# Softmax maxima written out by ScalarE instead of VectorE, in a decoder block on one Trainium2 core

## The chip, the cores and the metric

The kernel runs on one core of a Trainium2 chip. The core has five engines with queues of their own, each worked in order: TensorE (PE in the profile; PEld is its loading of weights), VectorE (DVE), ScalarE (ACT), GpSimd (POOL) and SyncE (SP), which here only issues DMAs. The metric is the device time of one execution in microseconds. Each profile comes from one further execution, whose own time is given beside it.

## What is computed

One decoder block on x, 32 batches of 128 tokens of width 256, in float32. The reference, cut to its frame:

```python
x = x + attn(layernorm(x), Wq, bq, Wk, bk, Wv, bv, Wo, bo)     # causal linear attention, 16 heads of 16
x = x + xattn(layernorm(x), ctx, ctx, Wq, Wk, Wv)              # softmax attention to a context of 128 tokens
x = x + ffn(layernorm(x), ...)                                 # silu gate, two gelu layers of 1024
```

The change is in the second line, where `attn = jax.nn.softmax(q k^T / 4)` over the 128 context tokens, for 16 heads. A softmax subtracts the maximum of each row of scores before the exponential. The kernel works on transposed scores (context token on the partition, query token along the free axis), so the negated maxima, which come out with the query token on the partition, have to be turned and then added to all 128 partitions.

## The kernel before, in words

**Work.** The batches go in 16 pairs. Each pair passes through linear attention (functions `a_...`, called "a" below) and, three pairs later (`SKEW` = 3), through softmax attention (`b_...`, called "b"). The feed-forward block (FFN) then works on 8 blocks of 4 batches, with weights kept in SBUF, and its matmuls in two parts (high and low, so that two float32r products give float32). All PE, ACT, DVE and POOL instructions stand in the order in which the program calls them (`tc.manual_schedule`, with all four engines in `ORDERED`); nothing is reordered.

**Order.** Lists written out by hand set that order. Each entry names a function, a pair offset and, where it applies, which batch of the pair (0 or 1, the first or second half). Functions are generators: each mention runs one up to its next `yield`. So `b_turn_maxima` stands twice for each half: at the first mention the PE transpose is emitted, at the second what comes after the `yield`, which is the part that the change touches. The lists in order of time: `head` and three `first` lists (linear attention alone), `both` (12 steps: linear attention of one pair and softmax attention of an earlier one), then `close`, `begins`, `alone` and `last` (one step each: the last four pairs of softmax attention), and `rest`. There are 32 halves: 24 in `both` and 2 in each of the four late lists. In `begins`, `alone` and `last`, `beside` and `settle` weave in the first FFN block: `beside` emits the matmuls of one FFN piece (`ffn_gate` L233 with a silu on ACT at L238, `ffn_gelu` L244 with a gelu at L248), and `settle` their ACT, DVE and POOL work, followed by `load_exp` (L81), a one-column Exp whose purpose is to bring back the table of Exp: so a table load to silu or gelu and a table load back (charged to L81) stand around each of these activations.

**One half of softmax attention.** `b_maxima` (L594): scores `sm` (L397), their negated maxima `nm` by two DVE reductions (L603), split into a float32r high part and a rest in the tile `z` (L607, L608). In `z`, group g (of four) has 32 columns; of these, columns 0 to 3 hold the high parts of its four heads i, 4 to 7 the rests, and the others are zero. `b_turn_maxima` (L611): PE transposes `z` into the PSUM tile `pz` (L613), so row 32g+i and row 32g+4+i hold head (g, i). These must go to four places: `mT` (L615) has four slots of 128 columns, and slot i keeps only the rows of head i, the others being zero. The column i of `sel` (L329) is one at the rows of head i and zero elsewhere. `b_scores` (L621): the scores once more, into `se` (L397), then per group a matmul with a matrix of ones (L628), whose 32 rows add up the rows of `mT` and so put minus the maximum on all 128 partitions; then ACT takes the exponential into `pr` (L639). `b_weighted` multiplies by the values (`pf`, L413), DVE turns the result (`fb`, L430), and `b_out` adds it to x (`pot` L652, `oc` L655).

**Other lines named below.** `phi` (L489) makes the features of linear attention: two Exp `e` (L495) and two Relu `r` (L497) on ACT. `b_queries`, `b_keys` and `b_values` copy projections out of PSUM on ACT (`qb` L571; `kb` L580 and L583; `vb` L592). `a_scores` masks scores on DVE (`at` L536); `a_values` writes `va` (L521) on DVE; `divided` turns `fa` and `fb` (L430). `ffn_input` casts `xh` on ACT (L188).

**Score banks.** The scores `sa` (linear attention), `sm` and `se` share two PSUM tiles (`ps_s`). The next scores can only be written when the last reader of the ones before is done: DVE's reduction after `sm`, ACT's exponential after `se`, DVE's masking after `sa`. The four other PSUM banks (`ps_m`) are given to all other tiles of the attention and, in the late lists, to the first FFN block.

Of the kernel before, what the change touches and what calls it, by code (L numbers as in the profile page):

```python
# [11 lines left out]
AF = mybir.ActivationFunctionType  # L12
ALU = mybir.AluOpType
# [3 lines left out]
P = 128  # L17
B, S, D = 32, 128, 256
# [26 lines left out]
def decoder_block_kernel(  # L45
# [14 lines left out]
    nc = tc.nc  # L60
# [207 lines left out]
    with tc.manual_schedule(engines=ORDERED):  # L268
# [7 lines left out]
        def buffer(shape, dtype, tag, name, **kw):  # L276
            side = att_a if tag in A_TAGS else att_b
            return side.tile(shape, dtype, tag=tag, name=name, **kw)
# [38 lines left out]
        sel = tiny.tile([P, 4], F32, name="sel")  # L317
# [16 lines left out]
        def bank(name):  # L334
            return ps_m.tile([P, 4, S], F32, tag="m", name=name)
# [275 lines left out]
        def b_turn_maxima(m, j):  # L611
            pz = bank("pz").rearrange("p a s -> p (a s)")[:, :S]
            nc.tensor.transpose(pz, Bs[m].pop(("z", j)).rearrange("p g r -> p (g r)"), ident)  # L613
            yield
            mT = buffer([P, 4, S], F32R, tag="mT", name="mT")  # L615
            nc.vector.tensor_tensor(
                mT, pz.unsqueeze(1).to_broadcast([P, 4, S]), sel.unsqueeze(2).to_broadcast([P, 4, S]), ALU.mult
            )
            Bs[m]["mT", j] = mT

        def b_scores(m, j):  # L621
# [60 lines left out]
        def settle():  # L682
# [42 lines left out]
        both = [  # L725
            (a_transpose, 1), (b_maxima, 0, 0), (b_transpose, 1), (b_values, 1), (b_maxima, 0, 0),
            (b_out, -1, 1), (a_scores, 0, 0), (a_transpose, 1), (b_transpose, 1), (b_turn_maxima, 0, 0),
            (a_scores, 0, 0), (b_out, -1, 1), (a_keys, 1), (b_values, 1), (b_turn_maxima, 0, 0),
            (w_load, 0), (norms, 0), (a_out, -1, 1), (b_scores, 0, 0), (a_keys, 1), (b_queries, 1),
            (a_out, -1, 1), (b_scores, 0, 0), (b_queries, 1), (b_maxima, 0, 1), (norms, 0),  # L730
            (b_weighted, 0, 0), (b_out, -1, 1), (b_queries, 1), (norms, 0), (b_maxima, 0, 1),
            (a_keys, 1), (b_load, 2), (a_weighted, 0, 0), (a_scores, 0, 1), (b_turn_maxima, 0, 1),
            (a_bias, 1), (norms, 0), (norms, 0), (b_weighted, 0, 0), (a_scores, 0, 1),
            (b_turn_maxima, 0, 1), (a_weighted, 0, 0), (b_weighted, 0, 0), (a_queries, 1),
# [318 lines left out]
```

## Time and profile before

| | |
|---|---|
| time, median of 3 runs | 1091.75 us (1090.9 to 1091.82) |
| time of the profiled execution | 1090.88 us |
| its span | 1088.7 us |
| granted TensorE clock, mean | 0.999 |
| multiply `mT` (L616) on DVE | 32 times, 681 ns in the mean, 21.8 us |
| transpose `pz` (L613) on PE | 32 times, 320 ns in the mean |
| negated maxima `nm` (L603) on DVE | 64 times, 1217 ns in the mean |
| exponentials `pr` (L639) on ACT | 64 times, 1020 ns in the mean |
| table loads on ACT | 15 at L238, 11 at L248, 12 at L81, 1283 ns each |

The span reaches from the first to the last instruction of the profiled execution; the time has some 2 us around it. A group in the profile is given as its line, engine, operation, tiles out<-in, shapes and count, then busy us, mean ns of one, and the idle time of the engine just before it with what ended it. In a timeline, the first number is the start in us from the start of the span, the second how long the row lasts, and brackets hold idle time before it with its releaser. The ends of matmuls are modelled. The stages lie as follows: `both` to about 370 us, `close` to 391, `begins` from there to 414, `alone` to 434, `last` to 455, then `rest` and the FFN blocks up to the end.

### The profile page before, as it was taken

The numbers are of one execution on the slowest core, as the hardware profiler recorded it, in microseconds if no ns is written. First come the engines' busy times: TensorE is split into PE (matmuls) and PEld (weight loads), VectorE is DVE, ScalarE is ACT, GpSimd is POOL, SyncE is SP. The second block draws the span as 40 slices with busy tenths as digits, with TensorE's granted clock in tenths as the row PEclk, the third lists the DMA queues.
The fourth block names the chain that finished last, engine by engine and source line by source line (L and its number), as shares of the span: only waits on it lengthen the run. The fifth ranks groups of instructions, "written<-read, shape, count | busy, mean of one in ns | idle before, by whom it ended". The sixth has DMA issues, their size and how long they took to land.

```text
span 1088.7 us, 19303 instructions
## 1 busy us (share of the span) xinstructions
PE 1076.1 (99%) x7990; PEld 875.4 (80%) x7990; DVE 598.7 (55%) x1209; ACT 377.8 (35%) x594; POOL 406.4 (37%) x649
## 2 busy tenths in 40 slices
PE   8999999999999999999999999999999999999998
PEld 6777777777777777778888888888888888888887
DVE  5888888888888876523433433433433432422422
ACT  3244444444444359822322322322312312312311
POOL 5554555545444446552312312312312312312311
PEclk9999999999999999999999999999999999999999
DMA  7011101111111000051011010011011000000000
GB/s 266 2 30 31 31 30 31 31 34 46 30 31 30 11 11 2 20 193 35 25 39 34 25 39 35 25 39 37 23 39 39 20 30 20 11 10 20 11 1 23
DMA packets 26542, 39.21 MB, mean 36 GB/s; under 512 B 2512, under 2 KB 18640, under 8 KB 26448
## 3 DMA queue, kind: packets, MB, share of 16 engines
q1 hardware_dynamic: 22000, 26.09, 7.3%
q0 software_dynamic: 4032, 11.54, 3.5%
q8 instruction: 65, 1.06, 0.4%
q10 hardware_dynamic: 416, 0.28, 0.1%
q14 instruction: 29, 0.24, 0.1%
HBM read 33.71 MB, written 4.19 MB: 35 GB/s over the span
## 4 chain that ended last, share of the span: by engine, by line
PE 94%; DVE 2%; POOL 1%; DMA 1%; issue 0%; ACT 0%; SPq 0%; POOLq 0%; DVEq 0%; ACTq 0%
PE ph L224 51%; PE pp L368 10%; PE py L877 6%; PE pf L413 5%; PE pv L376 5%; PE sa L397 4%; PE sm L397 3%; PE se L397 3%; PE pw L376 2%; PE pt L357 1%; PE pot L652 1%; DMA H<-in_h2T_dram 1%; PE se L628 1%; PE pz L613 1%; PE pt L213 1%; DVE at L536 1%
## 5 line engine op out<-in xcount | busy, mean ns | idle before, releaser
L189 DVE TENSOR_TENSOR gl<-hg,gh 128x512 fp32r<-128x512 f32 x125 | 86.9, 695 | 334.3 <-POOL gh L188 331.3
L248 ACT ACTIVATE hg<-ph,col 128x512 f32<-128x512 f32 x128 | 88.3, 690 | 362.5 <-PE ph L224 362.4
L188 POOL CAST gh<-hg 128x512 fp32r<-128x512 f32 x128 | 79.5, 621 | 357.9 <-ACT hg L248 357.9
L224 PE MATMUL ph<-gh,H 128*128 128x512 f32 x512 | 199.3, 389 | 0.5 <-POOL gh L188 0.5
L224 PE MATMUL ph<-sh,H 128*128 128x512 f32 x512 | 199.6, 390 | 0.0
L224 PE MATMUL ph<-gl,H 128*128 128x512 f32 x512 | 199.3, 389 | 0.2 <-DVE gl L189 0.2
L224 PE MATMUL ph<-sl,H 128*128 128x512 f32 x512 | 199.2, 389 | 0.0
L224 PEld LDWEIGHTS ph<-gh,H 128*128 128x128 f32 x512 | 96.1, 188 | 20.7 <-POOL gh L188 0.9
L224 PEld LDWEIGHTS ph<-gl,H 128*128 128x128 f32 x512 | 96.1, 188 | 20.5 <-DVE gl L189 0.5
L224 PEld LDWEIGHTS ph<-sh,H 128*128 128x128 f32 x512 | 96.1, 188 | 20.4 <-issue 0.5
L224 PEld LDWEIGHTS ph<-sl,H 128*128 128x128 f32 x512 | 96.1, 188 | 19.9
L224 PE MATMUL ph<-xh,W 128*128 128x512 f32 x256 | 100.7, 394 | 0.0
L224 PE MATMUL ph<-xl,W 128*128 128x512 f32 x256 | 99.8, 390 | 0.0
L603 DVE TENSOR_REDUCE nm<-sm 128x8 f32<-128x1024 f32 x64 | 75.2, 1217 | 17.9 <-PE sm L397 17.9
L188 POOL CAST sh<-hs 128x512 fp32r<-128x512 f32 x64 | 58.7, 917 | 68.6 <-DVE hs L240 68.6
L536 DVE TENSOR_TENSOR at<-sa,causal 128x1024 f32<-128x1024 f32 x64 | 74.5, 1206 | 14.6 <-PE sa L397 11.9
L639 ACT ACTIVATE pr<-se 128x1024 f32<-128x1024 f32 x64 | 62.0, 1020 | 29.6 <-PE se L628 29.6
L240 DVE SCALAR_TENSOR_TENSOR hs<-ph,col,sil 128x512 f32<-128x512 f32 x64 | 47.9, 749 | 41.3 <-PE ph L224 21.0
L238 ACT ACTIVATE sil<-ph,col 128x512 f32<-128x512 f32 x64 | 44.1, 690 | 74.9 <-PE ph L224 74.8
L495 ACT ACTIVATE e<-pp,col 128x256 f32<-128x256 f32 x64 | 26.9, 471 | 123.7 <-PE pp L368 92.7
L877 PE MATMUL py<-W,gh 128*128 128x256 f32 x256 | 62.6, 285 | 0.0
L877 PE MATMUL py<-W,gl 128*128 128x256 f32 x256 | 62.0, 283 | 0.0
(132 smaller groups left out, 1812.1 us busy)
## 6 DMA issues: line engine op xcount, KB each, us to landing
x<-in_x_dram SPq DMA_DIRECT2D x16, 256.0 KB, 5.5
cT<-in_ctxT_dram SPq DMA_DIRECT2D x16, 256.0 KB, 2.8
H<-in_h1T_dram POOLq DMA_DIRECT2D x8, 512.0 KB, 3.8
H<-in_h2T_dram POOLq DMA_DIRECT2D x8, 512.0 KB, 7.7
out_dram<-y SPq DMA_DIRECT2D x32, 128.0 KB, 1.7
raw<-in_h1T_dram SPq DMA_DIRECT2D x16, 256.0 KB, 2.7
raw<-in_h2T_dram SPq DMA_DIRECT2D x16, 256.0 KB, 2.6
WA<-in_wattn_dram SPq DMA_DIRECT2D x4, 256.0 KB, 4.8
```

The source lines that it names most:

```text
L188: (high_engine.copy if high_engine is nc.scalar else high_engine.tensor_copy)(high, t)
L189: lows.append(lambda: low_engine.tensor_tensor(low, t, high.bitcast(F32), ALU.subtract))
L224: nc.tensor.matmul(pp, lhsT=w[:, k, ts(c, P)], rhs=parts[p], start=(k == 0 and p == 0), stop=(k == len(src) - 1 and p == 1),)
L248: nc.scalar.activation(t, pp, AF.Gelu, scale=col[:, c_scale + c : c_scale + c + 1])
L368: nc.tensor.matmul(pp[:, c, :], lhsT=w[:, d, ts(c, P)], rhs=src[:, d, :], start=(d == 0), stop=(d == DC - 1))
L376: nc.tensor.matmul(pp, lhsT=src[:, d, :], rhs=w[:, d, :], start=(d == 0), stop=(d == DC - 1))
L397: nc.tensor.matmul(sc[g // 2][:, g % 2, 2 * c : 2 * c + 2, :], lhsT=loaded[32 * g : 32 * g + 32, c, ts(j, S)], rhs=streamed[32 * g : 32 * ...
L413: nc.tensor.matmul(pf[32 * g : 32 * g + 32, i, :], lhsT=v[:, 8 * (i // 2) + 2 * g + i % 2, :], rhs=weights[g // 2][:, g % 2, i, :], start= ...
L536: nc.vector.tensor_tensor(at.rearrange("p g i s -> p (g i) s"), sc[u].rearrange("p g i s -> p (g i) s"), causal.unsqueeze(1).to_broadcast( ...
L603: nc.vector.tensor_reduce(nm[:, 2 * u : 2 * u + 2, :], sc[u], AX.X, ALU.max, negate=True)
L639: nc.scalar.activation(pr, sc[u], AF.Exp)
L877: nc.tensor.matmul(py[:, :D], lhsT=h[k][p][:, ts(j, S)], rhs=W3[:, k, :], start=(k == 0 and p == 0), stop=(k == HC - 1 and p == 1),)
```

## The change

Where `b_turn_maxima` multiplied the turned maxima by all four columns of `sel` in one DVE instruction (128x512, with `pz` read four times by broadcast), it now issues four ACT activations of 128x128. Each reads `pz` and scales it by one column of `sel`, with the function Copy. They stand at the same place of the program, after the second mention of `b_turn_maxima`, but in ACT's queue. Nothing else is changed; line numbers after this place are one lower.

```diff
@@ b_turn_maxima
             nc.tensor.transpose(pz, Bs[m].pop(("z", j)).rearrange("p g r -> p (g r)"), ident)
             yield
             mT = buffer([P, 4, S], F32R, tag="mT", name="mT")
-            nc.vector.tensor_tensor(
-                mT, pz.unsqueeze(1).to_broadcast([P, 4, S]), sel.unsqueeze(2).to_broadcast([P, 4, S]), ALU.mult
-            )
+            for i in range(4):
+                nc.scalar.activation(mT[:, i, :], pz, AF.Copy, scale=sel[:, i : i + 1])
             Bs[m]["mT", j] = mT
```

## The prediction, on record before the run

> **What bounds the kernel now.** I read the engine totals of the page first, then busy time stage by stage, then the waits of VectorE and of the weight loads in the attention stage, then the timeline around single maxima steps, once in the steady stage and once in each late stage.
>
> ```profile
> PE 1076.1 (99%) x7990; PEld 875.4 (80%) x7990; DVE 598.7 (55%) x1209; ACT 377.8 (35%) x594; POOL 406.4 (37%) x649
> ```
> ```profile
> 63.00:376.00 313.00, 312.65 (x3639) 243.02 (x3632) 272.33 (x572) 138.74 (x251) 157.80 (x262) 1.00 0.11 32
> ...
> 414.00:434.00 20.00, 20.00 (x190) 14.79 (x188) 13.89 (x26) 18.95 (x26) 13.10 (x22) 1.00 0.01 1
> ```
>
> TensorE (PE) is busy 99% of the span, so the time changes only where PE's fixed order is made to wait longer or less. The second fence has, after the length of the stretch, busy us of PE, weight loads, VectorE (DVE), ScalarE (ACT) and GpSimd. Up to 376 us (the 12 steps of the list `both`, with 24 of the 32 maxima steps, 25.9 us a pair, and the start of `close`) DVE has 272 of 313 us and ACT 139. From 414 to 434 us it is the reverse: ACT has 18.95 of 20 us and DVE 13.89. The edit takes work from an engine that is full in one stage and puts it on one that is full in the other.
>
> Does DVE hold PE in the steady stage? In that stage's waits DVE itself waits for PE twice in every pair:
>
> ```profile
> DVE nm L603 <- PE sm L397: 8.8, 22, 1.4
> DVE va L521 <- PE pv L376: 8.5, 12, 0.7
> ```
>
> One pair's second half, in the timeline (start, length):
>
> ```profile
> 152.25 0.33 PE L613 MATMUL pz<-ident,z 128*128 128x128 f32 x1
> ...
> 154.35 0.84 ACT L495 ACTIVATE e<-pp,col 128x256 f32<-128x256 f32 x2 [6.06 <-PE pp L368]
> ...
> 155.19 0.68 DVE L616 TENSOR_TENSOR mT<-pz,sel 128x512 fp32r<-128x512 f32 x1
> ...
> 156.72 0.20 PEld L628 LDWEIGHTS se<-mT,ones 32*128 32x128 f32 x4
> ```
>
> The multiply stands behind two masking multiplies on DVE, ends at 155.87, and is needed at 156.72. ACT is idle for 6.06 us at that point.
>
> **What is removed.** 32 DVE multiplies of 0.681 us, 21.8 us. Nothing else on DVE, GpSimd or SyncE changes, and no DMA is moved.
>
> **What is added.** 128 ACT activations on 128x128 from PSUM with a column as scale. No such row exists. Nearest rows (ACT, 63 to 390 us):
>
> ```profile
> L497 ACT ACTIVATE r<-pp,col 128x256 f32<-128x256 f32 x48 | 20.2, 479 | 0.0
> L583 ACT ACTIVATE kb<-pp,col 128x512 f32<-128x512 f32 x26 | 16.8, 712 | 0.0
> L655 ACT COPY oc<-pot 128x256 f32<-128x256 f32 x24 | 8.9, 373 | 22.7 <-PE pot L652 22.7
> L580 ACT COPY kb<-pp 128x512 f32<-128x512 f32 x13 | 7.7, 592 | 0.0
> ```
>
> Plain copies give (592-373)/256 = 0.86 ns a column, so 0.263 us at 128. A column operand adds 0.10 to 0.12 us (479-373, 712-592). One is therefore 0.37 us. Two `r` follow each other in 0.84 us, not 0.96, so neighbours overlap by about 0.10: four take 3x0.27+0.37 = **1.18 us** against 0.69 now; I work with 1.15, and ACT is free for a following activation 1.05 us after it began. Bounds: the 128x1 activation of L81 takes 0.20 us, so four are at least 0.8; four of 0.47 (the 256 row, no overlap) are 1.9.
>
> [...]
>
> **Steady stage, 24 steps.** The four go into ACT's queue where the step's second part stands: ahead of the exponentials `e` of the next projection (second half: after `qb`; first half: after `vb`). Second half: pz ends at 152.58, the four run 152.7 to 153.85, `e` starts at 154.35 anyway, because it waits for PE; `mT` is ready 2.0 us sooner than now. First half: pz ends at 167.77, four to 169.0, `e` at 169.59; the old `mT` ended at 170.50. So `e` is not pushed, at 1.9 us by about 0.2, which the 0.54 and 1.51 us of ACT idle time before the softmax exponentials `pr` take up. On DVE, what stands behind the multiply comes 0.68 us sooner, and then waits for PE at `nm` or `va` as now. I count 0. Bound below nothing: weight loads wait for `mT` (4.0 us in all) and for `fa`, the next thing behind it (2.4 us), so at best -6.4 us. But those are gaps of 0.33 and 0.20 us, the same as the gaps with no releaser beside them, so I take the end at 0.
>
> **Late stages, 8 steps.** From 403 us on the first FFN block is woven in. ACT then holds, between pz and the exponentials, a table load, a silu (last step: gelu), the load back to Exp with its tiny `warms` activation, and then `pr`:
>
> ```profile
> 408.11 1.28 ACT L238 ACT_TABLE_LOAD   x1
> ...
> 409.15 0.27 PE L613 MATMUL pz<-ident,z 128*128 128x128 f32 x1
> ...
> 409.40 0.69 ACT L238 ACTIVATE sil<-ph,col 128x512 f32<-128x512 f32 x1
> 409.46 0.69 DVE L616 TENSOR_TENSOR mT<-pz,sel 128x512 fp32r<-128x512 f32 x1 [0.80 <-PE pz L613]
> ...
> 410.11 1.28 ACT L81 ACT_TABLE_LOAD   x1
> ...
> 411.51 1.92 ACT L639 ACTIVATE pr<-se 128x1024 f32<-128x1024 f32 x2
> ...
> 412.86 0.30 PEld L397 LDWEIGHTS sm<-kb,qb 32*128 32x128 f32 x4 [0.35 <-ACT pr L639]
> ```
>
> Here the change adds a wait. In the new order the four stand *ahead* of the load and silu, so ACT stops for pz, then runs the four, and only then starts the 3.41 us from that load to `pr` (408.11 or 418.19 to 411.51 or 421.60). Now it starts them before pz. PE's next maxima matmuls `sm` need the score banks that `pr` frees, and already wait for it (0.35 and 0.32 us). Step by step, each in the time of before, with 0.1 us from pz's end to ACT:
>
> 1. `close`, first: ACT idle before; only the four are longer. `mT` at 377.75, needed at 377.29: **+0.5**.
> 2. `close`, second: `qb`, `kb` move behind the four, `pr` from 388.89 to 389.25; its second bank is free at 391.2, and `sm` asks for it at 391.5: 0.
> 3. `begins`, first: `mT` at 397.7, needed 398.03; the casts `xh` 0.7 late, free by `pr`: 0.
> 4. `begins`, second: four 409.52 to 410.57, then `qb` (0.61 with its gap), load at 411.18 instead of 408.11: `pr` and `sm` **+3.1**.
> 5. `alone`, first: pz ends 419.52, load at 420.78 instead of 418.19: **+2.6** at `sm` (422.90, 423.57).
> 6. `alone`, second: pz ends 428.46, load at 429.72 instead of 426.51, `pr` at 433.12, second bank free at 435.05. PE has other work first: 0.5 from the later `mT`, then `sm`'s second bank is asked for at 434.5: **+1.1**.
> 7. `last`, first: pz ends 438.69 (439.8 with step 6's 1.1, and ACT catches up before it). The load, now at 436.12, comes at 441.06, `pr` at 444.47, done 446.41; the weighted sum `pf` (now 442.31, with 1.1 443.4) waits for both `pr`: **+3.0**.
> 8. `last`, second: pz ends 449.02, the four to 450.27, load, gelu, load, `warms`: `pr` at 453.7 instead of 450.87. PE runs 16 FFN matmuls first; `pf` from 454.30 to 455.6: **+1.3**.
>
> The sum is 0.5+3.1+2.6+1.1+3.0+1.3 = **+11.6 us**. PE is gapless from there to the end, so nothing gives it back. The profiled execution has a span of 1088.7 us and a time of 1090.88, so 1102.5 by it; the median of the three runs is 0.87 higher, so **1103.3**. Bounds of the four (0.8 to 1.9) enter six terms: -0.35x6 = -2.1, and +0.73x6 = +4.4 with about 1 more from terms 2 and 3: 9.5 to 17. With the -6.4 of the steady stage at the lower end, 1095 to 1109.
>
> **Rivals.**
> - *DVE is the bound of the steady stage* (faster). Place: DVE's queue from 63 to 376 us; price: 0.68 us a step, 24 times, -16.3, with +11.6 left -4.7, about 1087. For it: 87% busy, and PE's weight loads name DVE as releaser. Against: DVE waits for PE before `nm` and `va` in each pair, which a bound engine would not. It decides if more than 0.48 us (11.6/24) a step reach PE. Chance 0.05.
> - *No difference*: part of that gain and the late loss cancel, within 2 us of 1092. It takes some 0.4 us a step from DVE, with the same evidence against it. Chance 0.05.
> - *Small activations are dear*: if the cost is nearly all fixed, four at the spacing of the 512 rows (0.58) are 2.45 us. Six late terms grow by 1.3 each, and in the steady stage's first half `e` starts 0.6 late, just over `pr`'s 0.54: some +20, about 1113. Against it: 0.20 us for 128x1. Chance 0.08.
> - *The forecast*, 0.82: 1103.3.
>
> Range 1097 to 1110: the bounds of the four, and half of the steady stage's possible gain. About 0.2% (2.2 us) is what a measurement of this kernel can tell from no change. Slower 0.90 (the forecast and the dear activations), within 0.2% 0.05, faster 0.05.
>
> **What would show it.** Step length up to 376 us unchanged (25.9 us), `mT` done earlier there, DVE's idle time before `nm` and `va` longer. In 408 to 456 us, ACT idle before the first of the four, waiting for pz; `sm` or `pf` waiting for `pr` for some 3 us at steps 4, 5 and 7; PE idle some 11 us more between 376 and 460 us. Wrong if the steady steps get shorter by over 0.1 us, or if the four take more than 1.9 us.

## The result, and the profile after

| | before | after |
|---|---|---|
| time, median | 1091.78 us (1090.9 to 1091.85, 4 runs) | 1107.33 us (1104.52 to 1108.93, 4 runs) |
| profiled execution, time and span | 1090.88, 1088.7 us | 1108.46, 1106.4 us |
| granted TensorE clock, mean of that execution | 0.999 | 0.993 |

The changed kernel is slower: the ratio of the times is 1.0141, with an interval of 1.0128 to 1.0153. That is 15.5 us, where the forecast had 11.6. The runs after also differ more among themselves (by 4.4 us, against 1 us before). Of the 17 runs of before that stand beside experiments 5 to 8, two were slow (1337.84 and 1524.95 us, at mean clocks of 0.752 and 0.654), and no ratio here includes them.

The page of the changed kernel, its engine totals, the row of the granted clock in 40 slices, and the group of the new activations:

```profile
PE 1085.1 (98%) x7990; PEld 880.5 (80%) x7990; DVE 579.2 (52%) x1177; ACT 413.3 (37%) x722; POOL 405.3 (37%) x649
...
PEclk9999999999999998899999999999999999999999
...
L617 ACT ACTIVATE mT<-pz,sel 128x128 fp32r<-128x128 f32 x128 | 36.5, 368 | 81.0 <-PE pz L613 81.0
```

VectorE lost 19.5 us and 32 instructions, ScalarE gained 35.5 us and 128, as meant. Two things are new. PE has 9.0 us *more* busy time with the same 7990 instructions, and two slices of the clock row, the 16th and 17th (some 415 to 470 us), stand at 8.

**The steady stage.** The same stretch of the changed kernel that the prediction showed of before:

```profile
63.00:376.00 313.00, 312.65 (x3638) 243.40 (x3639) 257.98 (x549) 166.20 (x347) 157.55 (x262) 1.00 0.10 32
```

DVE went from 272.33 to 257.98 us and ACT from 138.74 to 166.20; PE has the same 312.65. From the first `pz` after 63 us to the one at 334 us, before takes 269.96 us and after 269.98. DVE's waits there, after:

```profile
DVE va L521 <- PE pv L376: 15.7, 12, 1.3
DVE nm L603 <- PE sm L397: 15.5, 22, 2.0
```

They were 8.5 and 8.8: the time that DVE saved, it waits. The prediction's small hope was 4.0 us in which weight loads waited for `mT`. Those rows of before, and then of after:

```profile
PEld se L397 <- DVE mT L616: 4.0, 12, 0.3
```
```profile
PEld se L397 <- DVE fa L430: 4.0, 12, 0.3
```

The gap has the same size and count with another name beside it, and the stage takes the same time: the name was that of the last event near the gap, and there was nothing to be won. What makes the gap is not shown.

**The late stages.** The timeline of the changed kernel around step 4 (`begins`, second half):

```profile
409.67 0.28 PE L613 MATMUL pz<-ident,z 128*128 128x128 f32 x1
409.98 1.14 ACT L617 ACTIVATE mT<-pz,sel 128x128 fp32r<-128x128 f32 x4 [1.99 <-PE pz L613]
410.99 0.60 ACT L571 COPY qb<-pp 128x512 f32<-128x512 f32 x1
...
411.62 1.28 ACT L238 ACT_TABLE_LOAD   x1
412.91 0.69 ACT L238 ACTIVATE sil<-ph,col 128x512 f32<-128x512 f32 x1
413.62 1.28 ACT L81 ACT_TABLE_LOAD   x1
415.02 1.92 ACT L638 ACTIVATE pr<-se 128x1024 f32<-128x1024 f32 x2
416.07 0.30 PEld L397 LDWEIGHTS sm<-kb,qb 32*128 32x128 f32 x4 [1.67 <-ACT pr L638]
416.99 0.73 PEld L397 LDWEIGHTS sm<-kb,qb 32*128 32x128 f32 x12 [0.61 <-ACT pr L638]
```

ACT stands still for 1.99 us until `pz` is there, runs the four in 1.14 us, and only then begins the chain of load, silu, load and `pr`. The silu starts 0.01 us after its load has ended (411.62 + 1.28, and 412.91), and the two loads, with the silu of 0.69 us between them, stand 2.00 us apart. The load was at 408.11 before and is at 411.62 now; the two waits of `sm` for `pr` grew from 0.35 and 0.32 to 1.67 and 0.61. What all of PE waits for between 391 and 480 us, after (before, the last row was the only one):

```profile
PE pf L413 <- ACT pr L638: 2.8, 3, 1.9
PE sm L397 <- ACT pr L638: 2.5, 4, 1.2
PE sm L397 <- ACT qb L571: 1.3, 1, 1.3
PE se L627 <- ACT mT L617: 0.8, 5, 0.2
PE pot L651 <- DVE oTb L445: 0.7, 1, 0.7
PE ph L224 <- ACT sil L238: 0.7, 1, 0.7
PE pz L613 <- DVE hs L240: 0.5, 1, 0.5
```

That is 9.3 us against 0.5, mostly for `pr`, as forecast. But 17.7 us of span are to be explained. The rest shows in the clock. Stretches of the changed kernel, as in the second fence of the prediction: length, busy us of PE, weight loads, DVE, ACT and POOL, and then the granted clock:

```profile
411.26:414.67 3.41, 2.75 (x14) 1.62 (x14) 1.04 (x2) 3.36 (x4) 0.23 (x1) 1.00 0.02 5
414.67:418.08 3.41, 1.97 (x21) 1.03 (x21) 2.11 (x8) 3.38 (x6) 3.33 (x5) 1.00 0.00 0
418.08:421.50 3.42, 3.42 (x38) 2.67 (x37) 3.35 (x6) 2.59 (x4) 3.09 (x8) 0.50 0.00 0
421.50:424.90 3.40, 3.40 (x23) 2.67 (x25) 0.89 (x3) 0.82 (x2) 2.63 (x4) 1.00 0.00 0
428.32:431.74 3.42, 1.68 (x16) 1.01 (x18) 0.61 (x2) 3.41 (x6) 2.14 (x3) 1.00 0.00 0
431.74:435.15 3.41, 3.41 (x40) 2.33 (x38) 2.70 (x4) 1.89 (x4) 0.46 (x1) 0.50 0.02 5
...
441.97:445.38 3.41, 2.09 (x19) 1.46 (x21) 1.77 (x6) 3.38 (x7) 2.90 (x6) 1.00 0.01 2
452.20:455.62 3.42, 1.54 (x10) 0.85 (x8) 1.10 (x2) 3.39 (x5) 1.82 (x2) 1.00 0.21 68
455.62:459.03 3.41, 2.92 (x38) 1.95 (x38) 0.79 (x2) 3.36 (x4) 0.05 (x1) 0.50 0.03 9
459.03:462.45 3.42, 3.42 (x20) 2.33 (x19) 2.43 (x4) 0.94 (x3) 3.14 (x4) 0.50 0.21 77
```

The clock is exactly 0.50 for whole stretches of 3.41 us, and 1.00 on both sides. Each of the three drops follows a stretch in which PE was busy for 1.54 to 1.97 of 3.41 us. The late lists of before have no such stretch: there PE is busy for 83.3 of the 84 us from 376 to 460 us at a clock of 1.00, the stretch 414 to 434 shown in the prediction among them.

**Where the 17.7 us of span came from.** I took the same PE instruction in both traces, at each place where PE waits, and read off how much the shift between the traces grew there.

| step of the prediction | forecast | measured |
|---|---|---|
| start-up differs by so much, whatever the kernel | 0 | 0.29 |
| 24 steps of `both` | 0 | 0.0 |
| 1 `close`, first | 0.5 | 0.26 |
| 2 `close`, second | 0 | 0.0 |
| 3 `begins`, first | 0 | 0.0 |
| 4 `begins`, second | 3.1 | 2.96 |
| half clock until the next `pz` (at 419.25 before, 424.35 after) | none | 1.59 |
| 5 `alone`, first | 2.6 | 2.52 |
| half clock until the next `pz` (at 428.19 before, 437.37 after) | none | 1.56 |
| 6 `alone`, second | 1.1 | 1.82 |
| 7 `last`, first | 3.0 | 2.85 |
| half clock until the next `pz` (at 448.69 before, 465.29 after) | none | 2.75 |
| 8 `last`, second | 1.3 | 1.13 |
| sum of steps 1 to 8 | 11.6 | 11.54 |
| sum of the three half-clock rows | none | 5.90 |

11.54 + 5.90 + 0.29 = 17.73 us. Four half-clock stretches of 3.41 us could cost at most half of 13.6, which is 6.8 us: an estimate, from the matmul `ph` of 128x512 that took 0.80 us at 460.76 us, at a clock of 0.50, and 0.39 us from 462.56 us on, behind the last drop.

### The profile page after: what moved, and what is told of

It is laid out like the page before. It is cut to its first block, busy times and chain, and to the rows that moved or that the text cites. A ratio compares the mean times of both kernels' runs of the same rounds, so it can differ in the third digit from the quotient of the medians.

```text
span 1106.4 us, 19398 instructions
## 1 busy us (share of the span) xinstructions
PE 1085.1 (98%) x7990; PEld 880.5 (80%) x7990; DVE 579.2 (52%) x1177; ACT 413.3 (37%) x722; POOL 405.3 (37%) x649
## 3 DMA queue, kind: packets, MB, share of 16 engines
q0 software_dynamic: 4032, 11.54, 3.3%
## 4 chain that ended last, share of the span: by engine, by line
PE 91%; ACT 3%; DVE 2%; POOL 1%; DMA 1%; issue 1%; SPq 0%; POOLq 0%; DVEq 0%; ACTq 0%
PE ph L224 50%; PE pp L368 10%; PE py L876 6%; PE pf L413 5%; PE pv L376 5%; PE sa L397 4%; PE sm L397 3%; PE se L397 3%; PE pw L376 2%; PE pt L357 1%; DMA H<-in_h2T_dram 1%; ACT pr L638 1%; PE pot L651 1%; PE pz L613 1%; PE pt L213 1%
## 5 line engine op out<-in xcount | busy, mean ns | idle before, releaser
L617 ACT ACTIVATE mT<-pz,sel 128x128 fp32r<-128x128 f32 x128 | 36.5, 368 | 81.0 <-PE pz L613 81.0
```

## The experiments

**Theory:** the eight late halves cost what the prediction worked out, because the four stand ahead of the load and silu in ScalarE's queue, and the idle time that this makes on PE then halves its clock, which costs the rest. **Rivals:** the excess comes from the steady stage; the four are simply too long, wherever they stand; or the excess is in something else that the late halves do.

**1. The steady stage alone.** The new activations only in `both` and before, the multiply in the four late lists:

```diff
-            for i in range(4):
-                nc.scalar.activation(mT[:, i, :], pz, AF.Copy, scale=sel[:, i : i + 1])
+            if m < 12:
+                for i in range(4):
+                    nc.scalar.activation(mT[:, i, :], pz, AF.Copy, scale=sel[:, i : i + 1])
+            else:
+                nc.vector.tensor_tensor(...)
```

> The four activations in the 24 steady halves alone (pairs 0 to 11), the VectorE multiply kept in the 8 late ones. Theory A (all of the loss comes from ScalarE's queue in the late halves, where the four stand ahead of the table loads, and from the TensorE clock that the new idle time loses): nothing changes, 1091.8 within 1 us, clock 0.999, and 25.9 us a pair as before. Rival B (VectorE or ScalarE work in the steady stage matters, in either direction, and the late halves cost more or less than they seem): over 2 us away from 1091.8.

Measured: 1091.55 us against 1091.34 for before on the same chip, ratio 1.0001 (0.9991 to 1.0011). 24 of 32 steps changed nothing. The rival of a bound DVE, which would have given 16 us here, is out, and so is any share of the steady stage in the loss above the 1.2 us that the interval leaves.

**2. The late stages alone.** The same with `if m >= 12`.

> The four activations in the 8 late halves alone (pairs 12 to 15). Theory A: as the whole change, some 1103 at the full clock and up to 1109 with what the clock loses: the span less its lost clock time ((1 - granted clock) x span) is about 1100 in every run. Rival B: visibly different from the whole change, under 1101 or over 1111.

Measured: 1108.42 us (1108.32 to 1108.52), ratio 1.0156 (1.0139 to 1.0173), at a mean clock of 0.991 to 0.994. The eight late halves are all of it.

**3. The wait without the length, first attempt.** The multiply stays on DVE; behind it ScalarE gets one activation on 128x1 that reads `pz` into a spare tile, so that it waits where the four waited:

```diff
             nc.vector.tensor_tensor(mT, ...)
+            if m >= 12:
+                nc.scalar.activation(warm, pz[:, 0:1], AF.Copy, scale=sel[:, 0:1])
```

> The kernel before, with the multiply on VectorE, and in the 8 late halves one tiny ScalarE activation (128x1, some 0.2 us) at the place of the four, which reads pz: the wait without the length. Theory A splits the order loss into the wait for pz ahead of the table load and the length of the four: the load starts late by 2.1 us at begins' second half, 1.6 and 2.2 at alone's, 2.1 and 0.4 at last's, where the weighted sum or the maxima matmuls wait for the exponentials, so about +7, 1099, and up to 3 more where the clock drops. Rival C (it is the length of the four that costs, the queue would have run ahead little anyway): +1 to +2, 1093 to 1094.

Measured: 1109.89 us, ratio 1.017 (1.0153 to 1.0187). This missed by some 10 us, because it didn't do what it was meant to. Its timeline at step 4:

```profile
410.26 0.27 PE L613 MATMUL pz<-ident,z 128*128 128x128 f32 x1
410.57 0.69 DVE L616 TENSOR_TENSOR mT<-pz,sel 128x512 fp32r<-128x512 f32 x1 [0.82 <-PE pz L613]
411.35 0.26 ACT L620 ACTIVATE warms<-pz,sel 128x1 f32<-128x1 f32 x1 [2.81 <-DVE mT L616]
```

The small activation, second reader of the PSUM tile `pz`, came to wait for the first reader too, the multiply, and so ended 1.08 us after `pz`. The four of the changed kernel end 1.17 us after theirs. So 0.26 us of work on ScalarE, let go at this moment, cost as much as 1.14 us there, and the clock fell here too (0.992 to 0.994 in the four runs). As a split of wait and length it tells nothing; experiment 9 repairs it.

**4. The length without the wait.** The multiply stays on DVE; ScalarE gets four activations of nearly the size (128x120), which read a constant in SBUF, write a tile that nobody reads and wait for nothing:

```diff
+            if m >= 12:
+                for i in range(4):
+                    nc.scalar.activation(aside, ident[:, :120], AF.Copy, scale=sel[:, i : i + 1])
```

> The kernel before, and in the 8 late halves four ScalarE activations of 128x120 with a column of sel as scale that read a constant and write a tile that nothing reads: the length without the wait for pz. Theory A: ScalarE, nearly full there, gets about 1.05 us later at each of the halves where the maxima matmuls already wait for the exponentials, and takes up part of it in its idle time: +3 to +4, about 1095, hardly any clock lost. Rival C (length is what costs): as the whole change without the clock, +9 to +12, 1101 to 1104.

Measured: 1097.7 us (1095.84 to 1097.92), ratio 1.0053 (1.0036 to 1.0069), 6.4 us more where 3 to 4 were expected. Steps 4, 5, 6 and 7 gave 1.4, 1.6, 0.3 and 2.05 us, read from `pz` to `pz`. The group between 408 and 460 us (five of the halves):

```profile
L621 ACT ACTIVATE edge<-ident,sel 128x120 f32<-128x120 f32 x20 | 8.0, 398 | 0.5
```

So in three of these four halves 1.6 us of plain work on ScalarE cost about its whole length: the late lists have less room there than I allowed for. Two things make the 6.4 us too large as a price of the change's length. These four hardly overlap, so they take 1.6 us where the changed kernel's take 1.14. And of the 7.0 us by which this profile's span exceeds that of before, 1.6 were there already at 350 us, from start-up; the late halves cost 5.4. There is no half-clock stretch in this profile between 400 and 485 us.

**5. The idle time filled.** The changed kernel with 58 matmuls of 128x128 (`ident` by `ident`) more, whose results are overwritten, put on PE where it idles, ahead of the pieces that the waits hold up:

```diff
-    def hidden(w, src, c):
+    def hidden(w, src, c, fill=0):
         ...
+        for _ in range(fill):
+            nc.tensor.matmul(pp[:, :S], lhsT=ident, rhs=ident, start=True, stop=True)
...
+            for _ in range(ahead):
+                nc.tensor.matmul(whole_bank[:, 3 * S :], lhsT=ident, rhs=ident, start=True, stop=True)
```

(`fill` is 12, 10 and 18 at gate pieces 2, 5 and 7, and 6 at gelu piece 1. The last two lines stand at `pot` of step 4, with 5 ahead of its matmuls and as many lines with 7 behind them.)

> The changed kernel, with 58 dummy matmuls (128x128 of a constant by itself, into parts of PSUM banks that are written afterwards or never read) put on TensorE just ahead of the places in the late steps where it now waits: 12, 10 and 18 ahead of the third, sixth and eighth gate piece, 12 around one transpose of the attention output, 6 ahead of the second gelu piece. They keep TensorE busy in idle time and do nothing else. Theory A (part of the loss is the clock, which drops because TensorE idles): the clock is granted in full, 0.999, the time is at +11.7, 1103.5 within 1.5 us and hardly spreads from run to run. Rival D (the clock drops for another reason, or the half clock costs nothing because ScalarE sets the pace there): 1105 to 1110 with the spread of the whole change, or longer by the dummies.

**6. The changed kernel once more, beside it,** with no edit.

> The changed kernel once more, beside the others on the same chip. Theory A: 1104 to 1109 with a wide spread, and in each run the span less its lost clock time ((1 - granted clock) x span) is 1099 to 1101. Rival D: the spread doesn't go with the clock.

Measured: 1104.87 us (1104.25 to 1105.48), ratio 1.0126 (1.011 to 1.0141), with the filling; 1108.7 us (1105.27 to 1109.05), ratio 1.0149 (1.0135 to 1.0163), without. More work on the engine that bounds the kernel made it 3.8 us shorter, between the medians (the fastest run without, 1105.27, lies among those with it). The same two stretches of the filled kernel, and then of the changed one in the same chip's run:

```profile
415.00:440.00 25.00, 24.68 (x236) 19.43 (x235) 13.50 (x26) 20.70 (x33) 13.45 (x20) 1.00 0.01 2
440.00:475.00 35.00, 34.22 (x307) 26.55 (x306) 13.76 (x33) 26.62 (x39) 18.58 (x30) 1.00 0.05 16
```
```profile
415.00:440.00 25.00, 21.47 (x180) 14.43 (x178) 12.15 (x24) 17.49 (x30) 12.50 (x19) 0.86 0.00 1
440.00:475.00 35.00, 30.18 (x248) 21.02 (x245) 15.02 (x34) 27.79 (x40) 17.07 (x27) 0.90 0.05 16
```

Clock 1.00 against 0.86 and 0.90. (Of the 543 matmul records against 428 in the same 60 us, 92 are the filling itself.) So the drops come from the idle time, and not from the new order as such.

The filled kernel also tests the ledger, since its order is the same at the full clock. From `pz` to `pz`, its steps 4 and 5 grew by 2.97 and 2.53 us, where the ledger has 2.96 and 2.52 besides the clock. Its steps 6 and 7 grew by 2.64 and 3.95, which is 0.8 and 1.1 us more than the ledger: there the filling takes 2.40 and 4.29 us and is longer than the wait that it fills (1.3 us for `qb` in step 6). 1104.87 therefore is not the price of the order alone, and the 3.8 us are less than the clock's share. With these 1.9 us added it is about 5.7 us (an estimate), close to the ledger's 5.90.

The unfilled kernel's runs spread roughly with their clock: 1107.0 us of span at 0.991, 1105.2 at 0.995, 1103.2 at 0.995 too. The products of span and clock are 1096.7 to 1099.7, somewhat under the 1099 to 1101 that I expected. The mean clock also counts half-clock stretches that have nothing to do with the late halves: the profile of this run has one from 19.51 to 22.92 us, in start-up, and those of experiments 1, 2, 4, 8 and 10 have one like it. Across it, each of these kernels falls back by 0.6 to 1.0 us against the profile of before (their first `pz` starts at 64.6 to 65.3 us, and at 63.5 to 64.0 in before, the first profile of the changed kernel and experiments 3 and 9), so a part of the spread from run to run comes from start-up.

**7. The same work in another place.** In the halves from step 4 on, the four are put behind the silu (or gelu) and ahead of the load back to Exp; in `last`, one `settle` is moved ahead of the scores to keep that order (the last line of the diff stands in `settle`, ahead of `load_exp`):

```diff
+            def write():
+                for i in range(4):
+                    nc.scalar.activation(mT[:, i, :], pz, AF.Copy, scale=sel[:, i : i + 1])
+            if (m, j) >= (13, 1): turned.append(write)
+            else: write()
...
+            while turned: turned.pop(0)()
```

> The changed kernel with the four activations, from the second half of pair 13 on, put behind the silu or gelu that they stood ahead of, and ahead of the load back to Exp (for one half, settle is called one entry sooner). The same work on ScalarE, but the load and silu can again run before pz is there. Theory A: what is left is the length of the four, about 1.15, 1.15, 0.6, 1.0, 0.9 and 0.25 us, +5, about 1097, clock 0.998 or more. Rival C (the length or the number of instructions on ScalarE costs, wherever they stand): little change from 1104 to 1109.

Measured: 1095.38 us (1094.29 to 1096.1), ratio 1.0038 (1.0025 to 1.005). All 128 activations are still on ScalarE, and 12 of the 15.5 us are gone. Its ScalarE at step 4:

```profile
408.35 1.28 ACT L238 ACT_TABLE_LOAD   x1
409.64 0.69 ACT L238 ACTIVATE sil<-ph,col 128x512 f32<-128x512 f32 x1
410.23 1.14 ACT L620 ACTIVATE mT<-pz,sel 128x128 fp32r<-128x128 f32 x4
411.38 1.28 ACT L81 ACT_TABLE_LOAD   x1
412.79 1.92 ACT L646 ACTIVATE pr<-se 128x1024 f32<-128x1024 f32 x2
```

The load runs while PE still makes `pz` (409.39 to 409.66 us), the four follow the silu and wait for nothing (no bracket), and `pr` starts at 412.79 instead of 415.02. What is left, 3.8 us, shows in part as waits of the matmul with ones for the later `mT` (2.1 us between 391 and 470 us, none before); the waits of PE before `sm` are gone, and the mean clock of its profile is 1.000. Copy worked with the table of either function: no load stands between `sil`, the four and the load to Exp that was there before.

**8. The other direction.** If ScalarE is full in the late lists and DVE is not, relief of ScalarE should help *before*. Two copies there go to DVE (`qb` of pair 14, `vb` of pair 15), and in `last` two mentions of the weighted sum go behind the turned maxima:

```diff
-            nc.scalar.copy(q, pp)
+            nc.vector.tensor_copy(q, pp) if m == 14 else nc.scalar.copy(q, pp)
...
-            nc.scalar.copy(v[:, :, :, 0:HD], pv)
+            (nc.vector.tensor_copy if m == 15 else nc.scalar.copy)(v[:, :, :, 0:HD], pv)
...
-            (b_weighted, -1, 1), (b_weighted, -1, 1), (b_turn_maxima, 0, 0), (b_turn_maxima, 0, 0),
+            (b_turn_maxima, 0, 0), (b_turn_maxima, 0, 0), (b_weighted, -1, 1), (b_weighted, -1, 1),
```

> The other way round: the kernel before, and in the late steps two PSUM copies (qb of pair 14, vb of pair 15) go from ScalarE to VectorE, and in the first half of the last step the turned result of the half before is asked for after the turned maxima and not before. Theory A: ScalarE's chain up to the exponentials, for which the maxima matmuls wait a little in begins and alone, gets 0.6 us shorter twice, and a wait of 0.45 us goes: -0.5 to -1.7, 1090 to 1091.3. Rival E (those waits are gaps that TensorE has anyway): 1091.8.

Measured: 1089.89 us (1088.65 to 1091.19) against 1091.62, ratio 0.9986 (0.9978 to 0.9995). It beats both kernels by a small but distinct amount, 1.7 us against before, a little more than expected (1090 to 1091.3). In `last`, first half, the matmul with ones no longer waits for `mT`. Before, and then in this kernel:

```profile
439.81 0.19 PEld L628 LDWEIGHTS se<-mT,ones 32*128 32x128 f32 x4 [0.45 <-DVE mT L616]
```
```profile
439.46 0.19 PEld L628 LDWEIGHTS se<-mT,ones 32*128 32x128 f32 x4
```

What each of the three edits gives by itself was not tried.

**9. The wait without the length, mended.** As 3, with the small activation ahead of the multiply, so that it waits for PE alone:

```diff
+            if m >= 12:
+                nc.scalar.activation(warm, pz[:, 0:1], AF.Copy, scale=sel[:, 0:1])
             nc.vector.tensor_tensor(mT, ...)
```

> As e3, but the tiny activation stands ahead of VectorE's multiply in the program, so that it waits for pz alone and not for the multiply too (in e3 it came to wait for both and started 0.8 us later); the multiply now waits for it, some 0.3 us. Theory A: the load starts late by 2.2, 1.7, 2.3, 2.1 and 0.4 us at the five late halves where that counts; begins +2.2, alone +1.7 and +1.0 (the maxima matmuls wait for qb, which stands behind the exponentials), last +2.1 and +0.4, close +0.3: +7.7, and 0 to 4 for the clock, 1099.5 to 1103.5. Rival C (the length of the four costs): +1 to +2, 1093 to 1094.

Measured: 1098.17 us (1097.67 to 1099.87), ratio 1.0068 (1.0055 to 1.0082): 6.7 us for activations of 0.26 us. Its timeline at step 4:

```profile
409.56 0.26 ACT L617 ACTIVATE warms<-pz,sel 128x1 f32<-128x1 f32 x1 [2.06 <-PE pz L613]
...
410.32 1.28 ACT L238 ACT_TABLE_LOAD   x1
...
413.73 1.92 ACT L641 ACTIVATE pr<-se 128x1024 f32<-128x1024 f32 x2
```

ScalarE loses 2.06 us here in one piece, and `pr` is late by about as much (411.51 before). From `pz` to `pz`, steps 4 to 7 grew by 2.2, 1.7, 0.95 and 2.1 us, each as expected; the median lies 1.3 us under the expected range, which had up to 4 us for the clock. The rival by which a wait alone is worth 1 to 2 us in all, and the length carries the loss, is out. The mean clock is 0.999: idle times of this size did not bring the clock down in the profiled execution (from 413.60 to 417.00 us PE has 2.00 us of work in 3.40, and the clock is 1.00 there and behind it).

**10. One half alone.** The four only in step 4, the multiply everywhere else:

```diff
-            for i in range(4):
+            if (m, j) == (13, 1):
+                for i in range(4): ...
+            else:
+                nc.vector.tensor_tensor(...)
```

> The four activations at one half only, the second of pair 13 (in begins), VectorE's multiply everywhere else. Theory A: each late half costs by itself: +3.0, 1094.6, and up to 1.7 more if the clock drops after the idle time, so 1094.5 to 1096.5. Rival F (a single delay is taken up by the steps that follow, and only the row of delays costs): under 1093.

Measured: 1095.27 us (1094.55 to 1097.26) against 1091.43, ratio 1.004 (1.0027 to 1.0054). One of the 32 steps costs 3.8 us. In its profile, the way from this `pz` to the next is 14.65 us instead of 10.10, and the three after it are as before (8.95, 10.17 and 10.33 us); 3.0 of the 4.55 is the order, and the clock, which falls right behind the step, is the rest:

```profile
410.28 1.14 ACT L618 ACTIVATE mT<-pz,sel 128x128 fp32r<-128x128 f32 x4 [1.99 <-PE pz L613]
...
415.31 1.92 ACT L643 ACTIVATE pr<-se 128x1024 f32<-128x1024 f32 x2
```
```profile
414.41:417.82 3.41, 1.97 (x16) 1.06 (x16) 2.36 (x8) 3.38 (x6) 3.00 (x4) 1.00 0.00 0
417.82:421.24 3.42, 3.42 (x41) 2.22 (x36) 3.08 (x5) 3.15 (x4) 3.09 (x8) 0.50 0.00 0
```

## Why the prediction was right, and where it was short

The sign, the place and the order terms were right, with step 6 too small. That 1107.33 lies within 1097 to 1110 is partly luck: the room above 1103.3 was left for longer activations, which came out as priced, and a lost clock filled it, which was no term of the range.

- **What bounds it.** Right: PE's fixed order. DVE's 87% in the steady stage was no bound, and its own waits for PE said so; they took up all that was freed (experiment 1).
- **The price of the four.** 368 ns each and 1.14 us together, against 0.37 and 1.15, from the 256 and 512 column rows. At step 4 the first begins 0.03 us after the end of `pz` (409.95 and 409.98), where I had allowed 0.1. The rival of dear small activations is out.
- **Steady stage, 0.** Right. The end of the range that allowed 6.4 us of gain, because weight loads "wait" for `mT`, was empty: the wait only changed its name.
- **Late steps 4, 5, 7 and 8.** Right to 0.2 us each. The table load and silu lost their head start, as forecast; experiments 9 and 4 show that both the lost head start and the length count (6.7 us for a wait with 0.26 us of work, and 5.4 us in the late halves for a length of 1.6 without a wait), and experiment 7 that the order alone takes 12 us back.
- **Step 1** was 0.26, not 0.5: small.
- **Step 6** was mis-sized: 1.82, not 1.1. I looked at the score bank that `pr` frees. But the next scores read `qb`, whose copy stands behind that `pr` in ScalarE's queue, after the change (444.05 us) as before it (431.73). The changed kernel's timeline:

```profile
444.05 0.59 ACT L571 COPY qb<-pp 128x512 f32<-128x512 f32 x1
444.69 0.74 PEld L397 LDWEIGHTS sm<-kb,qb 32*128 32x128 f32 x16 [1.75 <-ACT qb L571]
```

- **The step that failed** is the one behind the sum: "PE is gapless from there to the end, so nothing gives it back." I priced idle time on PE at its own length and took the clock of before, 1.00, for given. In its place the runs showed that idle time is paid for again: behind three stretches of 3.41 us in which PE is only about half busy (1.54 to 1.97 us), the clock falls to 0.50 for one or two stretches more. That is 5.9 us of the profiled execution (the ledger), and 3.8 us between the medians of experiments 5 and 6, where the filling costs some 1.9 itself. It probably also explains most of why the kernel now spreads over 4.4 us: the profiles of the changed kernel and of experiments 2 and 6 all have the same four half-clock stretches in the late lists, and that faster runs have fewer is only inferred from their mean clock (0.997 at 1104.52 us, 0.992 at 1108.93).
- **What would show it.** I asked for some 11 us more of idle time on PE between 376 and 460 us. From 376 us to the same instruction (467.3 before, 485.0 after) PE idles for 9.4 us against 0.7, and is busy for 99.6 against 90.6 with the same matmuls. The first is the wait; the second is mostly the clock, a mean of 0.94 there. (Ends of matmuls are modelled, so some of a short wait is booked as busy; the ledger goes by starts.)

The drops begin at 418.08, 431.74 and 455.62 us, 13.66 and 23.88 apart, which are 4 and 7 times 3.41. The longest single wait before a drop was 1.9 us (453.47 to 455.35), and PE had been busy for 45 to 58% of the 3.41 us ahead of each.

**What stays open:** the exact condition of the drop. Behind the late halves of the changed kernel, windows with 1.54, 1.68 and 1.97 us of PE's work led to one, and 2.09 and 2.75 did not. But PE's busy time alone does not decide. In start-up the same profile has a window with only 1.48 us, and the clock stays at 1.00 in it and behind it:

```profile
15.30:18.72 3.42, 1.48 (x9) 1.07 (x7) 1.26 (x3) 2.04 (x5) 2.73 (x4) 1.00 1.09 384
18.72:22.13 3.41, 3.31 (x26) 2.52 (x28) 3.04 (x6) 0.20 (x1) 0.00 (x0) 1.00 1.01 357
```

Before has 1.65 us from 14.83 to 18.24 us, also with no drop, while experiment 1 has 1.47 us at the same place of the program (16.97 to 20.38) and drops. In experiment 3 a window with 2.40 us (431.06 to 434.47) led to a drop, and one with 1.81 (444.71 to 448.12) did not. What does decide is not shown; that idle time has a part in it is, by the filling of experiment 5.

## What to carry to other kernels

Before work is moved to an engine that is idle on average, look stage by stage at what stands *behind* its new place in that engine's queue: here instructions of 1.1 us that wait for a late operand held up 3.4 us of table loads and silu that used to run ahead of it, and the same instructions a few places later cost a quarter. Where TensorE is the bound and runs without gaps, price a new gap twice, once for its length and once for a possible stretch of 3.41 us at half clock behind it (here 1.6 us for each of the first two). A wait that has the same length as the gaps around it that name nobody is no wait to be won (here 0.33 us before `se`, with the multiply on DVE and without it).

## What the hardware showed that was not expected

- A TensorE that was busy for 1.54 to 1.97 of 3.41 us lost half of its clock in the next 3.41 us (once 6.8 us), with no single gap over 1.9 us; a window with 1.48 us in start-up cost it nothing. 58 useless matmuls took 3.8 us *off* the time.
- Two engines that read one PSUM tile came to read it one after the other in program order (experiment 3): the second reader waited for a multiply of 0.69 us that writes elsewhere. Put first, it waited for `pz` alone (experiment 9), and the multiply then waited for it, an activation of 0.26 us. Whether the program's synchronization or the memory orders them was not tried.
